# Holding back a group's gate products in two RWKV layers of a four-layer sequence model

## The chip, the cores and the metric

The program runs on one core of a Trainium2 chip. Its time is the device time of one execution in microseconds (us); where several runs are given, their median stands for them. The profile is of one execution of its own. The engines are called PE (TensorE, matrix products), DVE (VectorE), ACT (ScalarE), POOL (GpSimd) and SP (SyncE, which here only issues DMAs). Each works through its own queue in order.

## The reference

A batch of 16 sequences of 100 rows with 512 channels goes through four layers: a cross-attention (layer 0), an RWKV block (1), a transformer block with cross-attention and a feed-forward part (2), and a second RWKV block (3). All is float32. The change lies in the RWKV block, cut here to what matters:

```
xa = ln(x, ln1); sx = previous row - xa
xxx = tanh((xa + sx * maa_x) @ maa_w1).reshape(b, l, 5, 32) @ maa_w2     # five mixes
xk, xw, xv, xr, xg = xa + sx * (maa_stack + xxx)
w = exp(-exp(time_decay + tanh(xw @ td_w1) @ td_w2))
r, k, v = xr @ Wr.T, xk @ Wk.T, xv @ Wv.T
g = silu(xg @ Wg.T)                                # the gate
a = k[:, None] * v[None, :]                        # step by step along the rows
out = r @ (u * a + s);  s = a + w[:, None] * s
x1 = x + (groupnorm(out) * gn_w + gn_b) * g @ Wo.T
xc = ln(x1, ln2); sx2 = previous row - xc          # channel mixing
rr = sigmoid((xc + sx2 * ffn_maa_r) @ Wfr.T)
kk = square(relu((xc + sx2 * ffn_maa_k) @ Wfk.T))
return x1 + rr * (kk @ Wfv.T)
```

The gate `g` is needed only at the end of the time mixing, where it multiplies the normalised output ahead of `Wo`.

## The kernel before

The function `rwkv` writes one RWKV layer. The 16 sequences form four groups (0 to 3) of four, so a tile has 128 channels by 400 columns (four sequences of 100 steps), and there are four chunks of channels in a group. The recurrence is a scan along the 100 steps on DVE. It is cut into 128 units, 32 for each group and 8 for each chunk. The loop over `u` at the end of `rwkv` goes from -42 past 128, and each pass (called a slot here) writes the fixed work of one unit:

- `spread(u + 1)`: two pairs of products with `sel` on PE that lay out `v` in PSUM (`vb`), and a small copy from `s0r` on ACT. There are two `vb` tiles, so a spread waits for the scan two units before its own.
- `product(u)`: `vb` times `kr` on DVE.
- whatever an earlier slot has deferred (`slots.begin`), mostly readers of PSUM banks.
- `scan(u)`: two scans on DVE, and `a` times `rr` on POOL.
- in every other slot `gather`: eight products with `gat` into `acc`, and at a chunk's end its norm, spread over later slots.

Into these slots the rest is filled from a list, `pieces`. A piece has a cost in us, the first slot in which it may come, and a function that writes it. The list is gone through in order: `following(u)` gives the first piece whose slot has come, or the second half of a product chain that has begun. Each slot has a budget, `due` (2.37 in units 0 to 28, 2.75 up to unit 95, 3.5 then, 3.9 after the last unit, less a bit for the slot's fixed work), and pieces are written until it is used up. This fixes the order on PE, DVE, ACT and POOL, which keep the order in which instructions are written. The order of SP's DMAs is left to a scheduler.

`projections(g, base)` lists the pieces of a group's mixing, for group 1 at slot -10 and then every 32 slots: statistics (`stats`) on DVE, `root` on POOL, `normed` (the tiles `xn`) on ACT, `turned` (PE transposes, then `ext`, `sx`, `sm` and `xm` by ACT and POOL), `inner` (products with `maa_w1`, tanh into `z` and `tz`), `mixed` (products with `maa_w2`, read by DVE as `tm` and by POOL as `xj`), and the chains of four products with `Wk`, `Wv`, `Wr` and, last, with `Wg`. These last are the gates, `gate(co)` for four blocks of channels: tanh on ACT (`th`), then a product on DVE (`g`), then a store to DRAM (`dg`). `k`, `v`, `r` and the decay `w` are stored to DRAM too, and are loaded again by SP in `enter` and `repeat` in the layout of the scan (`kr`, `wr`, `rr`). `gates(C)` loads a chunk's gate (`gc`) once its scans are over. `through(("in", g))` in `enter` writes all of a group's pieces up to `r` that are still left.

`output` lists the `Wo` products of a group once its scans are over. `channel_stream` lists the channel mixing of groups 0 to 2 at slot 86, and of group 3 after the last unit.

Three PSUM banks serve all pieces in turn. When a bank's turn comes while its deferred reader is not written yet, the reader is written first.

The functions that the diff touches, and what calls them:

Of the kernel before, what the change touches and what calls it, by code (L numbers as in the profile page):

```python
# [16 lines left out]
NC = E // 128  # L17
# [18 lines left out]
def xattn_sequence(ctx: ExitStack, tc: tile.TileContext, d: dict, out: bass.AP):  # L36
# [599 lines left out]
    def rwkv(n, ws, next_weights, last):  # L636
# [6 lines left out]
        with ExitStack() as es:  # L643
# [88 lines left out]
            pieces = []  # L732

            begun = []
            added = {g: [] for g in range(NG)}
            cm = {}
            nws = {}

            def following(u):
                return next(  # L740
                    (p for p in pieces if (p[2] is begun[0] if begun else p[1] <= u)), None
                )

            def piece(us, fn, slot=-1000, tag=None):
                pieces.append((us, slot, fn, tag))

            def take(p):
                pieces.remove(p)
                p[2]()
                return p[0]  # L750
# [28 lines left out]
            def chain(us, slot, tag, before, ps, lhs, rhs, read):  # L779

                bank = []

                def half(i):
                    if i == 0:
                        for fn in before:
                            fn()
                        bank.append(slots.bank())
                        begun.append(second)
                    else:
                        begun.clear()  # L790
                    for c in (2 * i, 2 * i + 1):
                        mm(out=ps(bank[0]), lhsT=lhs(c), rhs=rhs(c), start=(c == 0), stop=(c == NC - 1))
                    if i:
                        read(bank[0])

                second = lambda: half(1)
                piece(us / 2, lambda: half(0), slot, tag)
                piece(us / 2, second, slot, tag)
# [54 lines left out]
            def projections(g, base):  # L853
# [6 lines left out]
                def store(t, c, tile):  # L860
                    nc.scalar.dma_start(out=to[t][c].rearrange("r p t -> (r p) t"), in_=tile)
# [48 lines left out]
                def inner(lo, hi):  # L910
                    p0, z = (0, "z0") if lo == 0 else (64, "tz")
                    rs = slice(p0, p0 + hi - lo)
                    chain(
                        2.7, late, None, soon, lambda ps: ps[rs, :T], lambda c: w1[:, c, lo:hi],
                        lambda c: st["xm"][:, c, :],
                        lambda ps: scalar.activation(st[z][rs, :], ps[rs, :T], AF.Tanh),
                    )
# [24 lines left out]
                def linear(f, w, co, read, tag):  # L942

                    before = mixes[f] if f >= 0 else soon
                    x = lambda c: xj[f][:, c, :] if f >= 0 else st["xm"][:, c, :]
                    chain(2.7, late, tag, before, lambda ps: ps[:, :T],
                          lambda c: w[:, c, co * 128 : (co + 1) * 128], x, read)

                def plain(f, w, t, co):
                    def read(ps):  # L950
                        out = stage(f"{t}_{nm}_{co}")
                        scalar.copy(out[:, :T], ps[:, :T])
                        store(t, co, out[:, :T])

                    linear(f, ws[w], co, read, ("in", g))
# [24 lines left out]
                def gate(co):  # L980
                    def read(ps):
                        th = two.tile([128, T], F32, tag="tm", bufs=4, name=f"th_{nm}_{co}")
                        scalar.activation(th, ps[:, :T], AF.Tanh, scale=0.5)

                        def product():
                            g2 = stage(f"g2_{nm}_{co}")[:, :T]
                            vector.scalar_tensor_tensor(g2, th, 1.0, ps[:, :T], ALU.add, ALU.mult)
                            store("g", co, g2)

                        slots.read_later(ps, product)  # L990

                    linear(4, ws["Wg"], co, read, None)
# [7 lines left out]
                    piece(0.45, lambda c=c: turned(c), base + 1)  # L1000
                late = base + 2
                mix = lambda fs, c: piece(0.75, lambda: mixed(fs, c), late)
                inner(0, 128)
                mix((0, 1), 0)
                mix((0, 1), 1)
                inner(128, 160)
                mix((0, 1), 2)
                mix((0, 1), 3)
                for c in range(NC):
                    plain(0, "Wk", "k", c)  # L1010
                    mix((2, 3), c)
# [7 lines left out]
                    plain(*((2, "Wv", "v", c + 2) if c < 2 else (3, "Wr", "r", c - 2)))  # L1019
                plain(3, "Wr", "r", 2)  # L1020
                plain(3, "Wr", "r", 3)
                for co in range(NC):
                    gate(co)

            def channels(g, slot):

# [83 lines left out]
                        i, slot, None, [], lambda c: st["kk"][:, c, :], lambda c: cm["Wfv"][:, c, :], read  # L1110
                    )

                def written(fn):
                    rest, pieces[:] = pieces[:], []
                    fn()
                    got, pieces[:] = pieces[:], rest
                    return got

                some = lambda fn, n: written(lambda: [piece(0.01, lambda i=i: fn(i), slot) for i in range(n)])
                root, normed = ln_apply(st, [xb[g * G + i] for i in range(G)], xn, nm)  # L1120
                return {
# [9 lines left out]
            def channel_stream(groups, slot):  # L1131

                got = []
                parts = [channels(g, slot) for g in groups]
                for k in ("stats", "normed", "turned"):
                    got += parts[0][k]
                for p, q in zip(parts, parts[1:] + [{"stats": [], "normed": [], "turned": []}]):
                    got += p["first"] + q["stats"] + p["second"] + q["normed"]
                    got += p["third"] + q["turned"] + p["fourth"]
                return got  # L1140
# [152 lines left out]
            UNITS = 32 * NG  # L1293
            u, due = -42, 0.0
            while u < UNITS + 6 or pieces or slots.due:
                slots.now = u
                g = (u + 10) // 32
                if u % 32 == 22 and g + 1 < NG:
                    projections(g + 1, u + 7)
                elif u % 32 == 22 and g + 1 == NG:  # L1300
                    pieces.extend(channel_stream(range(NG - 1), u + 7))
                elif u % 32 == 0 and u > 0:
                    if u == UNITS:

                        kept = max(len(pieces) - 4, 0)
                        for i in range(kept, len(pieces)):
                            pieces[i] = (pieces[i][0], u + 8, *pieces[i][2:])
                        own = channel_stream([NG - 1], u + 8)
                        pieces[kept:kept] = own[: G + 1]
                        pieces.extend(own[G + 1 :])  # L1310
                    output(g - 1, u + 7)
                if u == UNITS - 32 - 3:
                    cm.update(load(n, "Wfk", "Wfr", "Wfv"))
                if u >= UNITS and not nws and not any(p[3] == ("wo", NG - 1) for p in pieces):
                    nws.update(next_weights())
                unit = 0 <= u < UNITS
                if 0 <= u + 1 < UNITS:
                    spread(u + 1)
                if unit:
                    product(u)  # L1320
                slots.begin()
                if unit:
                    scan(u)
                C, at = u // 8 + 1, u % 8
                if 0 <= C < NC * NG:
                    if at == 4:
                        enter(C)
                    elif at == 6:
                        repeat(C, 1)
                        bonus(C, 0)  # L1330
                    elif at == 7:
                        bonus(C, 1)
                C = u // 8
                if 0 <= C < NC * NG and at == 2:
                    bonus(C, 2)
                if 0 < C <= NC * NG and at == 4:
                    gates(C - 1)
                if u % 2 and 0 <= (u - 3) // 2 < UNITS // 2:
                    gather((u - 3) // 2)

                due = min(due, 0.0) + (2.37 if 0 <= u < 29 else 2.75 if u < UNITS - 32 else 3.5 if u < UNITS else 3.9)
                due -= 0.45 * (u % 2) + 0.7 * (at in (2, 7)) if unit else 0.0
                for p in [p for p in pieces if p[0] == 0 and p[1] <= u]:
                    take(p)
                while due > 0:
                    p = following(u)
                    if p is None:
                        break
                    due -= take(p)
                u += 1  # L1350
# [359 lines left out]
    def load(layer, *names):  # L1710
        return {k: load_w(d[f"L{layer}_{k}"], f"l{layer}_{k}") for k in names}
# [75 lines left out]
```

## Time and profile before

| | us |
|---|---|
| median of three runs | 3452.1 (3450.18 to 3452.9) |
| profiled execution | 3447.39 |
| its span, first to last instruction | 3445.6 |
| PE busy in the span | 3121.5 |
| DVE busy | 1753.5 |
| POOL busy | 1373.2 |
| ACT busy | 977.3 |
| first scan of layer 1, last scan of layer 1 | 857.4, 1472.8 (its start) |
| first scan of layer 3, last scan of layer 3 | 2745.1, 3356.8 (its start) |

The mean granted clock of PE over the span is 0.942 of full speed.

How to read the lines that follow. A line of the timeline has the start in us from the span's beginning, the length, the engine, the source line, the operation, the tiles written and read, the shape and how many instructions were merged. In square brackets stands how long the engine was idle ahead of it, and what released it. Nearly all lines say L77 or L82, which are helpers that record every operation, so a group is told by its tiles. A product in float32 is recorded as two instructions. A line of a table of windows has the window, its length, then busy time and count of PE, PE's weight loads, DVE, ACT and POOL, then the granted clock, the share of DMA time and GB/s. A busy PE is not PE at its peak: with a halved clock or a late operand the recorded lengths grow.

### The profile page before, as it was taken

What the parts mean: (1) busy time and instruction counts of PE and PEld (TensorE: products, weight loads), DVE (VectorE), ACT (ScalarE), POOL (GpSimd) and SP (SyncE); (2) the same over time, 40 slices, a digit from 0 to 9 for tenths busy, and PEclk for the clock granted to TensorE, in tenths of its full rate; (3) what the DMA queues carried; (4) which work ended last, traced back from release to release, by engine and by line L of the source; (5) the groups of instructions that cost most, each with busy time, mean ns of one, the idle gap of its engine ahead of it and who ended that gap; (6) DMA issues with size and microseconds to landing.
All of it is one profiled execution on the core that took longest, in us unless ns stands there. A gap on an engine that the chain in (4) does not pass through costs nothing. (4 is left out here: it accounts for less than half of the span.)

```text
span 3445.6 us, 47937 instructions
## 1 busy us (share of the span) xinstructions
PE 3121.5 (91%) x18371; PEld 1422.0 (41%) x18371; DVE 1753.5 (51%) x3570; ACT 977.3 (28%) x1715; POOL 1373.2 (40%) x1036
## 2 busy tenths in 40 slices
PE   6989898868999989988999999879998899998997
PEld 3434443334333333334455555445553433333333
DVE  4777777732877766523333333320001287766661
ACT  1333233222233333321323222211111233423332
POOL 0444444443775765521212111220002377676551
PEclk8999999979999989999999999989998999998998
DMA  5010100013335353222000000010011343535321
GB/s 173 22 31 22 31 22 34 1 32 115 113 108 150 109 173 108 77 72 64 28 19 20 19 20 31 26 64 10 10 58 34 111 129 102 150 116 174 91 70 50
DMA packets 171374, 240.18 MB, mean 70 GB/s; under 512 B 27678, under 2 KB 139358, under 8 KB 171146
## 3 DMA queue, kind: packets, MB, share of 16 engines
q1 hardware_dynamic: 148106, 204.35, 19.9%
q10 hardware_dynamic: 23040, 32.78, 2.7%
q8 instruction: 144, 2.36, 0.3%
q14 instruction: 84, 0.69, 0.1%
HBM read 174.25 MB, written 36.04 MB: 61 GB/s over the span
## 5 line engine op out<-in xcount | busy, mean ns | idle before, releaser
L77 POOL TENSOR_TENSOR a<-a,rr 128x800 f32<-128x800 f32 x256 | 480.9, 1880 | 331.0 <-DVE a L77 212.0
L77 DVE TENSOR_TENSOR_SCAN a<-wr,vb 128x400 f32<-128x400 f32 x512 | 475.9, 971 | 20.7 <-PE acc L82 9.1
L77 DVE TENSOR_TENSOR vb<-vb,kr 128x792 f32<-128x792 f32 x256 | 250.1, 977 | 184.7 <-ACT vb L77 184.5
L77 DVE CUSTOM_DVE_ANT_0 junk<-l_sc,mask 100x361 f32<-100x361 f32 x512 | 272.9, 533 | 87.1 <-PE l_sc L82 70.5
L82 PE MATMUL vb<-vc,sel 32*128 32x396 f32 x1024 | 252.7, 565 | 3.3 <-DVE a L77 3.3
L77 DVE TENSOR_TENSOR pt<-l_sc,maskT 121x400 f32<-121x400 f32 x384 | 193.4, 566 | 89.6 <-PE l_sc L82 88.8
L77 ACT ACTIVATE pt<-pt 121x1600 f32<-121x1600 f32 x96 | 147.6, 1538 | 282.4 <-DVE pt L77 280.8
L1490 DVE CUSTOM_DVE_ANT_0 junk<-l2a_sc,mask 100x361 f32<-100x361 f32 x256 | 136.9, 535 | 173.0 <-PE l2a_sc L82 155.8
L1526 POOL TENSOR_TENSOR pa<-pt,pt 121x1600 f32<-121x1600 f32 x16 | 57.1, 3569 | 362.3 <-ACT pt L1521 362.3
L77 POOL TENSOR_TENSOR xj<-tm,ext 128x400 f32<-128x400 f32 x160 | 150.6, 961 | 110.9 <-DVE tm L77 110.1
L77 DVE SCALAR_TENSOR_TENSOR tm<-mm,vec,sx 128x400 f32<-128x400 f32 x160 | 95.7, 628 | 185.5 <-PE mm L82 149.4
L82 PE MATMUL k<-ct,l_k_w 128*128 128x361 f32 x512 | 173.3, 482 | 14.4 <-DMA ct<-in_ctxT 14.4
L1707 DVE TENSOR_TENSOR x<-pb,x 100x512 f32<-100x512 f32 x16 | 12.2, 760 | 335.4 <-DMA pb<-po 330.3
L77 POOL TENSOR_TENSOR pa<-pt,pt 121x1600 f32<-121x1600 f32 x32 | 114.7, 3583 | 165.0 <-ACT pt L77 165.0
L63 PE MATMUL h<-yTb,l_fc 128*128 128x400 f32 x512 | 174.5, 503 | 6.3 <-ACT yTb L229 6.3
L82 PE MATMUL v<-l_v_w,ct 128*121 128x512 f32 x384 | 175.5, 601 | 0.0
L63 PE MATMUL p<-l_proj,h 128*128 128x512 f32 x384 | 165.5, 592 | 0.0
L77 ACT COPY vb<-s0r 128x8 f32<-128x8 f32 x256 | 42.9, 168 | 407.8 <-PE vb L82 320.4
L82 PE MATMUL l_sc<-kz,qz 32*100 32x361 f32 x1024 | 116.7, 526 | 42.9 <-DVE pt L77 22.0
L82 PEld LDWEIGHTS vb<-vc,sel 32*128 32x128 f32 x1024 | 81.9, 191 | 154.0 <-issue 113.5
L63 PEld LDWEIGHTS h<-yTb,l_fc 128*128 128x128 f32 x512 | 97.7, 192 | 81.1 <-ACT yTb L229 8.3
L77 POOL TENSOR_TENSOR pa<-pa,pt 119x1600 f32<-119x1600 f32 x32 | 114.4, 3576 | 41.1 <-ACT pt L77 40.9
(258 smaller groups left out, 5174.2 us busy)
## 6 DMA issues: line engine op xcount, KB each, us to landing
kr<-dk SPq DMA_DIRECT2D x256, 100.0 KB
wr<-dw SPq DMA_DIRECT2D x256, 100.0 KB
rr<-dr SPq DMA_DIRECT2D x256, 100.0 KB
ct<-in_ctxT SPq DMA_DIRECT2D x32, 722.0 KB
dk<-k ACTq DMA_DIRECT2D x32, 200.0 KB
kc<-dk SPq DMA_DIRECT2D x32, 200.0 KB
dw<-wd ACTq DMA_DIRECT2D x32, 200.0 KB
dv<-v ACTq DMA_DIRECT2D x32, 200.0 KB
```

The source lines that it names most:

```text
L63: nc.tensor.matmul(out=ps, lhsT=lhs(c), rhs=rhs(c), start=(c == 0), stop=(c == n - 1))
L77: return lambda *args, **kw: tc.keep_in_program_order(op(*args, **kw))
L82: pin(nc.tensor.matmul(**kw))
L1490: nc.vector.tensor_tensor_reduce(out=junk, in0=ss[r][:L, :S2], in1=t["mask"], scale=-1.0, scalar=FLT_MAX, op0=ALU.add, op1=ALU.min, accum_ ...
L1526: nc.gpsimd.tensor_tensor(t["pa"], t["pt"][0], pt, ALU.add)
L1707: nc.vector.tensor_tensor(x, pb[:, i, :], x, ALU.add)
```

## The change

The four gate products of a group are no longer listed at the end of its own mixing. `projections` writes them into a list apart, `held`. The next call of `projections` puts them into its own pieces, one ahead of each of the first four parts: the first `inner`, two mixes, the second `inner`, two mixes. Their first slot is one before the new group's `base`, except for the first two that group 1 takes over, which may come at once. For the last group, `channel_stream` puts them behind its first `turned` pieces. Two budgets change. The helper `written` moves outward so that both callers reach it; it does what it did.

```diff
+            held = []
...
+            def written(fn):
+                rest, pieces[:] = pieces[:], []
+                fn()
+                got, pieces[:] = pieces[:], rest
+                return got
...
-                inner(0, 128)
-                mix((0, 1), 0)
-                mix((0, 1), 1)
-                inner(128, 160)
-                mix((0, 1), 2)
-                mix((0, 1), 3)
+                parts = [
+                    lambda: inner(0, 128), lambda: [mix((0, 1), c) for c in range(2)],
+                    lambda: inner(128, 160), lambda: [mix((0, 1), c) for c in range(2, 4)],
+                ]
+                for i, part in enumerate(parts):
+                    slot = base - 1 if g > 1 or i > 1 else -1000
+                    pieces.extend((p[0], slot, *p[2:]) for p in held[2 * i : 2 * i + 2])
+                    part()
...
-                for co in range(NC):
-                    gate(co)
+                held[:] = written(lambda: [gate(co) for co in range(NC)])
...
                 for k in ("stats", "normed", "turned"):
                     got += parts[0][k]
+                got += [(p[0], slot - 1, *p[2:]) for p in held]
+                held.clear()
...
-                due = min(due, 0.0) + (2.37 if 0 <= u < 29 else 2.75 if u < UNITS - 32 else 3.5 if u < UNITS else 3.9)
+                due = min(due, 0.0) + (2.22 if 0 <= u < 29 else 2.8 if u < UNITS - 32 else 3.5 if u < UNITS else 3.9)
```

In the built program, the order of the gate products around the slots in question is as follows. PE ahead of unit 0 keeps its order.

| slots | gate products before | after |
|---|---|---|
| 24 to 29 | all four of group 1 | the first two (28, 29) |
| 30, 31 | none | the third, half behind the transposes, half behind slot 31's gather |
| 35 | none | the fourth, between the second `inner` and the next mixes |
| 56 to 61 | all four of group 2 | the first two (60, 61) |
| 62, 63 and 66, 67 | none | the third; the fourth |
| 89 to 93 | all four of group 3 | the first two (92, 93) |
| 94, 95 and 96 | none | the third in halves behind the transposes and behind slot 95's gather; the fourth in 96 |

The pieces that follow come one to two slots later than before, and some of the channel mixing moves behind unit 125.

More of the change, by code (lines that the diff above doesn't have):

```diff
@@ L1111, in values @@
                     )
[L1113 to L1117, printed above, removed]
                 some = lambda fn, n: written(lambda: [piece(0.01, lambda i=i: fn(i), slot) for i in range(n)])
```

## Prediction

> **What bounds the kernel now.** I read the busy row and the clock row of the page, then a table of stages over the first RWKV layer, then the timeline at the places where that table loses time.
>
> ```profile
> PE 3121.5 (91%) x18371; PEld 1422.0 (41%) x18371; DVE 1753.5 (51%) x3570; ACT 977.3 (28%) x1715; POOL 1373.2 (40%) x1036
> ...
> PEclk8999999979999989999999999989998999998998
> ```
> ```profile
> 857.00:966.00 109.00, 104.87 (x427) 39.75 (x428) 91.91 (x115) 31.57 (x72) 78.52 (x63) 0.95 0.39 117
> 966.00:1005.00 39.00, 33.58 (x129) 13.25 (x128) 25.70 (x34) 14.41 (x30) 30.54 (x27) 0.86 0.33 95
> 1005.00:1111.00 106.00, 105.63 (x433) 40.84 (x432) 79.95 (x101) 32.54 (x70) 65.35 (x51) 0.97 0.46 136
> ...
> 1262.00:1305.00 43.00, 32.14 (x98) 13.05 (x96) 21.40 (x30) 17.84 (x34) 27.99 (x27) 0.72 0.60 194
> ```
>
> The first number after the window is its length, the next TensorE's busy time, and the share below 1 is the granted clock. In 1005 to 1111 TensorE is busy 105.63 of 106: it is the bound. In 966 to 1005 (group 1's mixing to group 2's) and 1262 to 1305 (the last group to the channel mixing) it is not: 5.4 and 10.9 us idle, at a clock of 0.86 and 0.72. The timeline of the first place:
>
> ```profile
> 970.92 0.93 PE L82 MATMUL vb<-vc,sel 32*128 32x396 f32 x4
> 971.79 0.88 PE L82 MATMUL acc<-a,gat 128*32 128x400 f32 x8
> 972.60 1.61 PE L82 MATMUL mm<-xj,l_Wg 128*128 128x400 f32 x4
> 974.14 0.93 PE L82 MATMUL vb<-vc,sel 32*128 32x396 f32 x4
> ...
> 978.24 0.56 PE L85 MATMUL mm<-ident,xn_a 100*128 100x100 f32 x4 [1.04 <-ACT ext L77]
> 981.42 1.70 PE L82 MATMUL mm<-rk,ones 128*128 128x400 f32 x2 [1.75 <-POOL rk L77]
> 985.85 5.21 PE L82 MATMUL mm<-xm,maa_w 128*128 128x400 f32 x8 [1.23 <-POOL xm L77]
> ```
> ```profile
> 982.00:986.00 4.00, 2.77 (x11) 0.36 (x9) 2.02 (x4) 2.51 (x4) 4.00 (x6) 0.50 0.87 267
> 986.00:990.00 4.00, 4.00 (x6) 1.98 (x7) 0.52 (x1) 0.00 (x0) 4.00 (x4) 0.50 0.69 164
> ```
>
> Starts give prices: a spread 0.87, a gather 0.81, half a product chain 1.54 (a whole one 2.88 by other rows). Transposes, shift, mix and the `maa_w` product follow each other through ACT, POOL and PE, and PE waits at each step.
>
> **The change, part by part.** No matrix product, vector operation or byte of DMA is added. I write slot u for unit u's pass of the loop. The built order shows what moves:
>
> (a) Ahead of unit 0, PE's order is the same. On VectorE the four statistics of group 1 stood behind all four gate products; now the last two stand behind `g` 1, and `th` 3 on ScalarE stands behind the four `xn`.
>
> ```profile
> 835.06 0.69 DVE L77 BATCH_NORM_STATS2 st_a<-x 100x6 f32<-100x512 f32 x1
> 838.44 0.23 POOL L77 TENSOR_SCALAR ve_a<-mv_a 100x4 f32<-100x4 f32 x1 [21.72 <-DVE mv_a L77]
> 840.44 2.93 ACT L77 ACTIVATE xn_a<-x,shift_a,rstd_a 100x512 f32<-100x512 f32 x4 [5.90 <-POOL shift_a L77]
> 841.31 0.43 PE L85 MATMUL mm<-ident,xn_a 100*128 100x100 f32 x1 [7.37 <-ACT xn_a L77]
> 843.28 0.61 ACT L77 ACTIVATE kc<-kc,vec 128x400 f32<-128x400 f32 x1
> ```
> `g` 1 ends at 829.8; two statistics at 0.86 end at 831.5; root and shift take 2.0 (838.44 to 840.44); `xn` runs 833.5 to 836.4 beside the last gate chains. Then `th` 3 (0.5), `g` 3 (0.57), its store's issue (0.33) are ahead of `kc`, which starts at 837.9 instead of 843.28: everything behind it, `ext` to unit 0, comes 5.4 earlier. Unit 0's loads don't hold it: the DMA share is 0.19 in 838 to 842 and 0.08 from 840. Two layers: 10.8.
>
> (b) At units 30 and 62. Before, from the spread at 970.92 to the end of the first half `Wk` product at 1006.3 are 35.4 us, for PE work of 6 spreads (5.2), 3 gathers (2.4), a half gate (1.5), 16 transposes (1.6), the `ones` product (0.9), `maa_w` (4.3), 8 mixes (3.5), the centring (0.8), half a `Wk` (1.5): 21.7, so 13.7 lost. The same stretch at the other three places (unit 62, and both in layer 3) loses 10.7 to 13.0; mean 12.6. After, three gates more stand in the stretch, and the preceding slots are as much emptier. I walk it from 970.92 with the same durations: gate 1 whole until 975.5; spread 976.4; the third transpose waits for gate 1's bank (`th` 976.4, `g` 977.0), the fourth for `ext` (978.4), end 978.8 as before. Half of gate 2 fills until 980.3, the spread until 981.2; `ones` waits 0.7 for `rk`, gather and gate 2's other half end at 985.1, a spread at 986.0. `xm` on POOL comes at 986.3 to 989.0, so `maa_w` ends at 989.7. Mixes, `maa_w`'s rest, centring, spread, `mean`, gather: 999.8; gate 3 until 1002.7; spread, four mixes (waiting for `tm` behind scan 36) and half a `Wk`: 1009.0. That is 38.1 for 31.6 of work (two spreads, a gather, `mean`, two and a half gates more): 6.5 lost. Gain 6.1 a place, but some 4.4 at unit 30: in group 0 VectorE is busy 92 of 109 us (first row of the stages) and PE not quite the bound, so of the 6.7 us of gates taken out of it I let 5 come back. Two layers: 21.0.
>
> (c) At unit 94.
> ```profile
> 1274.74 0.43 PE L85 MATMUL mm<-ident,xn_1b 100*128 100x100 f32 x1 [4.50 <-ACT xn_1b L77]
> ...
> 1289.89 3.54 PE L82 MATMUL mm<-xk_1b,l_Wfk 128*128 128x400 f32 x4 [4.57 <-POOL xk_1b L77]
> ```
> Four half gates (5.8) move behind the transposes, into the second wait. But the statistics come one unit later (behind `g`, a product and scan 94: 3.5 more), so the first wait grows from 4.5 to 8. The walk, from slot 93's spread: spread, gather and half a gate to 3.2, spread 4.1; scan 94 ends at 6.4, the statistics 9.8, root (on POOL behind `a` 94 and `rk`) 11.6, `xn` from 12.4, transposes 15.2; half a gate, spread, `ones`, gather, half a gate 20.8; spread and gate 3 to 24.6. POOL's eight mixes of 0.93 run from 19.2 to 26.7, so the first half of `Wfk` doesn't wait (26.1); spread 27.0, gather behind `a` 95 at 29.4, half a `Wfk` 30.9. Before, slot 97's spread begins at 37.6 (1304.53) with four half chains (5.5) more, but without that spread and gather (1.7): equal work is at 34.7 against 37.6. With 5.4 less ahead of it, 8.3. Two layers: 16.6.
>
> (d) The budgets (2.22 for 2.37 in units 0 to 28, 2.8 for 2.75) split chains otherwise; half a chain alone costs 0.2 more than in a whole. Summed by these prices, units and tail together hold 528 us of PE work by either order; some 6.8 us move behind unit 125. There one half product fills the wait of 4.2 for POOL's last `gc`: 1.5, two layers 3.
>
> (e) Queues. SP's order changes: `gc` loads move ahead of `kr` loads, as late as a gate's store. `Wr`'s last store comes 3 units later (unit 59 and 91); its row must land before unit 64 and 96, over 20 us later, against a store and 13 issues of 0.4: nothing. From group 1 on `gc` waits for buffers that `Wo` frees, as now.
>
> Sum: 51.4 at full clock. The clock's price: the rows of 982 to 990 show 0.50 though no PE wait there reaches 2 us. The Trainium skill, TensorE: Matmul & The Clock Gate, Part 1, puts the half rate behind an idle window of some 3.4 us. By that rule nothing in (b) drops after the change, and only (a) and (c) would pay. The row decides: the clock dropped in a stretch that was thinly filled (7.1 busy of 9), and the walk still has 2.4 us of waits between transposes. From 980 to 991 the granted clock is 0.53: 10.3 us at half rate, at most 5.1 of work lost, and each of the six places has such a row. I charge it whole at (c), with its wait of 8, and one in two at (b): 2 x 5.1 + 4 x 2.6 = 20.6. Gain 30.8.
>
> The profiled run took 3447.4 (span 3445.6, the rest outside it); the sums are made on it, and taken from the median of 3452.1, which is 4.7 longer with the same work: **3421.3**.
>
> **Rivals.** *Full clock*: no dip at these places, 3452.1 - 51.4 = 3400.7. For it: the gates are steady work; against: (a) keeps thin stretches. *Only the start gains*: the stalls return elsewhere since the mixing begins later by a unit, 3452.1 - 10.8 = 3441; for it, (c)'s longer first wait. *No effect*: 3452; against, PE's 7.37 is no other engine's limit. *Slower*: a held gate's `g` stands before a scan in VectorE's queue, and its `th` now behind four `sm` (gate 2) or two table loads (gate 3) on ScalarE. Behind the scan wait POOL's `a`, and the second next spread with all of PE. In the walk scan 32 frees that spread 0.8 before PE asks. Twelve such waits; beyond the 0.8 each us is on the path, so 2.6 more eat the 30.8, and at 3.6 more it is 3464.5. Such waits show 2.1 now (57.1 over 27), which leaves it the smaller case.
>
> **How the numbers follow.** 0.2% (6.9 us) is what a measurement here can tell from no change. Likeliest, with its dips up or down: 0.58, own range 3408 to 3438. Full clock 0.07, only the start 0.09 (of it some within 0.2%), no effect 0.08, slower 0.18. So faster 0.72, same 0.10, slower 0.18; the range 3400 to 3459 leaves out the far end of slower and little below.
>
> **What would show it.** (a) the first scan 5 us earlier; (b) the waits for `rk` and `xm` mostly gone, and a higher clock; (c) the wait for `xn_1b` longer, that for `xk_1b` under 1. It is wrong if `g` waits over 100 us in total, or if the clock in 966 to 1005's counterpart stays under 0.86.

## The result and the profile after

| | before | changed |
|---|---|---|
| median, us | 3452.4 | 3444.5 |
| ratio (95% interval) | | 0.9975 (0.9964 to 0.9986) |
| profiled execution, us | 3447.39 | 3446.68 |
| its span, us | 3445.6 | 3444.8 |
| PE busy in the span, us | 3121.5 | 3117.8 |

Both medians are of 20 executions. The change is real but small: 8.6 us of 3452 (4.8 to 12.4), where 30.8 were forecast. Executions of one kernel spread by some 10 us either way; the two profiled executions happen to lie 0.7 apart. So sizes below come from the ratios, as (1 - ratio) x 3452, and the traces tell the place.

The page of the changed kernel, busy row and clock row:

```profile
PE 3117.8 (91%) x18371; PEld 1421.2 (41%) x18371; DVE 1754.7 (51%) x3570; ACT 977.3 (28%) x1715; POOL 1373.0 (40%) x1036
...
PEclk8999999979999899899999999989998899999999
```

Its stages of layer 1 (columns as in the table of windows before):

```profile
851.00:965.00 114.00, 109.25 (x466) 42.25 (x466) 101.42 (x126) 40.21 (x87) 87.23 (x68) 1.00 0.39 119
965.00:1005.00 40.00, 37.56 (x140) 13.41 (x140) 27.05 (x36) 12.14 (x25) 32.56 (x30) 0.91 0.30 89
1005.00:1111.00 106.00, 97.92 (x412) 37.09 (x410) 77.07 (x97) 31.32 (x67) 62.19 (x49) 0.97 0.46 138
...
1160.00:1262.00 102.00, 93.67 (x386) 35.94 (x385) 71.28 (x85) 28.34 (x62) 59.11 (x45) 0.95 0.47 139
1262.00:1305.00 43.00, 33.74 (x128) 15.10 (x127) 24.56 (x35) 17.94 (x36) 28.57 (x27) 0.84 0.52 167
```

and of the kernel before the one stage that was not shown:

```profile
1160.00:1262.00 102.00, 102.00 (x423) 39.71 (x424) 75.08 (x90) 29.96 (x67) 63.16 (x48) 0.98 0.50 148
```

The two places that the prediction looked at are better: in the mixing's stretch PE is busy 37.56 of 40 at a clock of 0.91 (before 33.58 of 39 at 0.86), in the channel mixing's at 0.84 instead of 0.72. The two stretches behind the mixings, where PE was the bound, no longer are: 97.92 of 106 and 93.67 of 102, against 105.63 and 102.00. In these, 16 us of PE's time went missing in one layer, against 0.4 before. The starts of scans say it in time:

| start of unit's scan, us | before | changed | lead |
|---|---|---|---|
| layer 1, unit 0 | 857.4 | 851.4 | 6.0 |
| unit 28 | 968.3 | 952.2 | 16.1 |
| unit 36 | 1009.5 | 989.8 | 19.7 |
| unit 62 | 1125.4 | 1114.8 | 10.6 |
| unit 76 | 1193.7 | 1192.3 | 1.4 |
| unit 94 | 1273.1 | 1271.9 | 1.2 |
| unit 127 | 1472.8 | 1463.2 | 9.5 |
| layer 3, unit 0 | 2745.1 | 2737.0 | 8.1 |
| unit 36 | 2898.2 | 2879.5 | 18.7 |
| unit 94 | 3160.4 | 3159.4 | 1.0 |
| unit 127 | 3356.8 | 3351.6 | 5.2 |

The lead at unit 36 is there in both layers, and it is larger than what the prediction's steps (a) and (b) ask for by then (5.4 and 4.4; in layer 3, 3.7 of it stood before the layer began). It is nearly gone at unit 76. (Of unit 28's lead a part is only work put off by the smaller budget: in experiment 2, which has the budgets alone, a lead of 7.0 over the first scan at unit 30 has shrunk to 0.2 at unit 36.)

PE at the first mixing transition of the changed kernel, the counterpart of the timeline shown before:

```profile
961.11 1.25 PE L85 MATMUL mm<-ident,xn_a 100*128 100x100 f32 x12
963.12 0.56 PE L85 MATMUL mm<-ident,xn_a 100*128 100x100 f32 x4 [0.76 <-ACT ext L77]
963.70 1.61 PE L82 MATMUL mm<-xj,l_Wg 128*128 128x400 f32 x4
...
966.30 0.94 PE L82 MATMUL mm<-rk,ones 128*128 128x400 f32 x2
...
970.74 3.70 PE L82 MATMUL mm<-xm,maa_w 128*128 128x400 f32 x8 [0.29 <-POOL xm L77]
```

The waits of 1.75 for `rk` and 1.23 for `xm` are 0 and 0.29, and `maa_w`'s eight products take 3.70 instead of 5.21, at full clock. At the channel transition:

```profile
1279.87 0.43 PE L85 MATMUL mm<-ident,xn_1b 100*128 100x100 f32 x1 [8.19 <-ACT xn_1b L77]
...
1295.02 1.58 PE L82 MATMUL mm<-xk_1b,l_Wfk 128*128 128x400 f32 x4
```

the first wait is 8.19 (forecast: 8) and the second none (forecast: under 1). So the waits at these places are as the walks had them. What took the gain back are waits that the kernel before doesn't have. The first, at unit 46, seen on PE, POOL and SP:

```profile
1046.78 1.70 PE L82 MATMUL mm<-rk,ones 128*128 128x400 f32 x2 [5.78 <-POOL rk L77]
```
```profile
1041.04 1.03 POOL L77 TENSOR_TENSOR gc<-gc,og 128x400 f32<-128x400 f32 x1 [3.92 <-PE vb L82]
...
1045.68 1.04 POOL L77 TENSOR_TENSOR rk<-rc,kc 128x400 f32<-128x400 f32 x1
```
```profile
1028.96 4.21 SPq L837 DMA_DIRECT2D x<-ox  x6
...
1037.25 0.37 SPq L1275 DMA_DIRECT2D gc<-dg  x1
```

The gate's load `gc` stands behind six stores of `Wo`'s rows and eight loads on SP and is issued at 1037.25. POOL waits for it until 1041.04 (the profile puts the wait down to `vb`, whose products end at the same moment; experiment 7 issues the gates' loads by ACT and the wait is gone; it moves a row load too, but that one is not late here), and two mixes, an `a` and `rk` queue behind it, so PE's `ones` product waits 5.78. The second, at unit 76, on PE, DVE and SP:

```profile
1187.49 0.84 PE L82 MATMUL mm<-z,maa_w2a 32*128 32x400 f32 x4
1192.46 4.39 PE L82 MATMUL mm<-xj,l_Wk 128*128 128x400 f32 x8 [4.14 <-DVE ox L77]
```
```profile
1192.12 0.29 DVE L77 TENSOR_TENSOR ox<-mm,ox 128x128 f32<-128x128 f32 x1 [5.36 <-DMA ox<-x]
```
```profile
1184.13 1.65 SPq L837 DMA_DIRECT2D x<-ox  x2
...
1188.33 2.47 SPq L832 DMA_DIRECT2D ox<-x  x4
```

DVE adds `Wo`'s fourth row tile to the rows `ox`. These rows are loaded just ahead of use, DVE stands idle for 5.36 with a scan next in its queue, and a bank stays taken, so PE waits too. In SP's built order that load was far ahead in the kernel before (group 0's is row 72 of the queue and group 1's row 73); the change left the one in place and moved the other to row 202:

```
72   DMACopy ox_0_3<-x  32x128 x4      before and changed
73   DMACopy ox_1_3<-x  32x128 x4      before
202  DMACopy ox_1_3<-x  32x128 x4      changed
```

The traces have it so. SP's first row loads of layer 1, before and then changed:

```profile
743.27 5.00 SPq L823 DMA_DIRECT2D ox<-x  x8
```
```profile
743.53 2.47 SPq L832 DMA_DIRECT2D ox<-x  x4
```

What makes the load late is a store. It reads rows 68 to 99 of the group's last sequence, and `Wo`'s third row tile is stored into rows 0 to 83 of the same tile. Where the load is written ahead of that store, it depends on no result of the layer, and the scheduler puts it at the layer's head. Where it is written behind the store, SP has to wait for the store first; in the built program of the changed kernel such a wait stands just ahead of row 202. The lines show the round trip: the third tile's rows are stored at 1184.13, the load follows at 1188.33, and DVE adds at 1192.12. The kernel before writes load and use of groups 0 and 1 in one slot (44 and 76), and yet ahead of the store. In the changed kernel the four tiles of group 1 begin in slots 71, 72, 74 and 75 instead of 72, 73, 75 and 76, and the third is stored before the fourth begins.

The totals of DVE's waits, before and then changed:

```profile
DVE ox L77 <- DMA ox<-x: 10.6, 2, 5.3
```
```profile
DVE ox L77 <- DMA ox<-x: 20.4, 4, 5.4
```

The line has the idle time, how often, and the longest. Two waits (group 2's rows at unit 108, one in each layer) are in both kernels; the other two are new. That is as many as there are loads written behind such a store: over both layers two in the kernel before and in experiment 5, four in the changed kernel and in experiments 7 and 11, six in experiments 1, 6 and 8, and none in those that write the load earlier (9, 10, 13 to 16). (Experiment 2 has four, and waits for three.)

### The profile page after: what moved, and what is told of

The parts are those of the page before. It is cut to its first block, busy times and chain, and to the rows that moved or that the text cites. A ratio compares the mean times of both kernels' runs of the same rounds, so it can differ in the third digit from the quotient of the medians.

```text
span 3444.8 us, 47891 instructions
## 1 busy us (share of the span) xinstructions
PE 3117.8 (91%) x18371; PEld 1421.2 (41%) x18371; DVE 1754.7 (51%) x3570; ACT 977.3 (28%) x1715; POOL 1373.0 (40%) x1036
## 5 line engine op out<-in xcount | busy, mean ns | idle before, releaser
L82 PE MATMUL k<-ct,l_k_w 128*128 128x361 f32 x512 | 172.5, 480 | 13.5 <-DMA ct<-in_ctxT 13.5
```

The lines of the kernel that those rows point to most:

```text
L82: pin(nc.tensor.matmul(**kw))
```

## The experiments

Gains are given against the kernel before, as (1 - ratio) x 3452, with the interval of the ratio. "Old budgets" are 2.37 and 2.75, "new" ones 2.22 and 2.8.

**1. All gates held, old budgets.**

```diff
-  (2.22 if 0 <= u < 29 else 2.8 if ...
+  (2.37 if 0 <= u < 29 else 2.75 if ...
```

> The gates are held as in the changed kernel, but the budgets stay at 2.37 and 2.75. Theory A, waits of the new order (a held gate pushes every later piece of its group back, and the Wo rows, the chunk loads and the last mixes then meet SP's and POOL's queues badly): the lead of 20 us at unit 36 of layer 1 is there and is lost again by unit 76 and unit 125 as in the changed kernel, 3438 to 3452. Theory B, the budgets (2.22 puts off pieces of group 0, 2.8 draws the later ones forward, and that makes the waits): the lead is kept, 3420 to 3432.

Measured 3457.0, ratio 1.0018 (1.0008 to 1.0028): 6 slower than before, and outside both expectations. The new budgets are not what makes the waits; under the old ones the held gates fare worse. DVE waits for `ox` in every group but the last (41.3 in total, six times, up to 7.8), and at unit 95 PE waits 7.4 for `rk`, which stands behind eight mixes on POOL.

**2. The budgets alone**, in the kernel before (2.22 and 2.8, gates not held).

> The kernel before with the budgets 2.22 and 2.8 alone, gates not held. Theory A: about as before, 3445 to 3460. Theory B: the waits seen in the changed kernel (the ones product for rk at unit 47 near 6 us, the POOL mixes at unit 125) come without the held gates, and it is 12 to 22 slower, 3464 to 3474.

Measured 3502.3, 1.0150 (1.0134 to 1.0167): 52 slower, far outside both expectations. The budgets are a gain only together with the held gates; the prediction had them at 3 us of gain. Where the 52 go was not found: of the waits in its trace, PE's for `xm` stand at 25.9 (12.0 before) and those behind `ox` at 13.6 (none before), and both layers lose.

**3. Only group 0's gates held**, old budgets.

```diff
-  held[:] = written(lambda: [gate(co) for co in range(NC)])
+  if g == 0:
+      held[:] = written(lambda: [gate(co) for co in range(NC)])
+  else:
+      for co in range(NC):
+          gate(co)
```

> Only the gates of group 0 are held, and written into group 1's mixing; the gates of groups 1 to 3 stay behind their own group's chains; old budgets. Prediction's step (a): the first scan of each layer 5 to 8 us earlier and unit 7 to 9's half clock gone, 3441 if it stays. Theory A: the lead at unit 28 of 12 to 16 us is there, and what is left at the end is less than 6 a layer. Rival, the start is paid back before unit 30: as before, 3452.

Measured 3429.7, 0.9942 (0.9920 to 0.9964): 20.0 faster, more than the 3441 expected. Step (a) had 10.8 for both layers. Its profiled execution lies 17 above its median, so no size is read from that. A second part of the gain was looked for in the half clock behind the start. The kernel before runs at a clock of 0.57 in 884 to 896 (units 7 to 9), the changed one at full clock in the same units:

```profile
884.00:896.00 12.00, 12.00 (x34) 4.56 (x38) 6.82 (x9) 0.68 (x3) 7.34 (x5) 0.57 0.44 129
```
```profile
878.00:890.00 12.00, 12.00 (x59) 4.53 (x59) 10.65 (x14) 2.39 (x7) 9.93 (x8) 1.00 0.58 176
```

But the changed kernel has other budgets there. Experiment 5, with the start and the budgets of this one, has the half clock nearly whole, and its lead over the first scan does not grow in units 0 to 36 of that layer:

```profile
882.00:894.00 12.00, 12.00 (x37) 4.36 (x36) 6.64 (x10) 0.83 (x3) 6.80 (x5) 0.58 0.47 126
```

In this experiment's own trace it lasts 3.4 us instead of 10.2 and the lead grows by 3.3. So the half clock does not go with the held gates every time, and what makes 20.0 of 10.8 is open.

**4. Only group 3's gates held**, old budgets (the condition is `g == NG - 1`).

> Only the gates of group 3 are held, and written behind the transposes of the channel mixing; groups 0 to 2 as before; old budgets. Prediction's step (c): 8.3 at full clock less 5.1 for the clock at each of two places, so 3446, with the wait for xn_1b near 8 and that for xk_1b under 1. Theory A: the gain at unit 96 is there and the last mixes at unit 125 take it back: 3450 to 3458. A rival, the clock: no gain at unit 96 either, since the wait of 8 costs as much in half clock as the fill brings.

Measured 3434.2, 0.9955 (0.9941 to 0.9970): 15.5 faster, near step (c)'s 16.6 at full clock and not its 6.4 with the clock's charge. Both waits were as forecast.

**5. Groups 0 and 3 held, 1 and 2 not**, old budgets.

> The gates of group 0 and of group 3 are held, those of groups 1 and 2 are not; old budgets. If the two gains measured apart add up: 22.6 + 18.1 less than before, 3412. If each was partly one run's luck with the clock, or if both save the same idle time: 3425 to 3432. In either case the changed kernel would be slower than this by what it pays for groups 1 and 2.

Measured 3416.6, 0.9901 (0.9884 to 0.9918): 34.2 faster, nearly the sum of the two (35.5), and 26 better than the whole change.

**6. Only groups 1 and 2 held**, old budgets: step (b) by itself.

> Only the gates of groups 1 and 2 are held, so only the mixing at units 30 and 62 changes; old budgets. Prediction's step (b): 21.0 less 10.4 for the clock, 3442. Theory A': the transition gains at units 30 to 36 as predicted, but the order behind it makes the row load of the Wo rows (ox) stand behind the chunk loads on SP, with some 7.6 of DVE idle at units 44 and 76 in each layer (30 together, less the gain of 21): about 3460. By difference (all held with old budgets +4.7, start -22.6, channels -18.1): +45, 3497.

Measured 3461.1, 1.0023 (1.0011 to 1.0035): 7.9 slower, as theory A' had it (its place and its size; the cause is the store described above, not a place behind the chunk loads). The place is the one of theory A', on DVE

```profile
1048.67 0.29 DVE L77 TENSOR_TENSOR ox<-mm,ox 128x128 f32<-128x128 f32 x1 [7.64 <-DMA ox<-x]
```

and on PE, 7.74 behind it:

```profile
1040.34 0.94 PE L82 MATMUL mm<-z,maa_w2a 32*128 32x400 f32 x4
1049.02 5.33 PE L82 MATMUL mm<-xj,l_Wk 128*128 128x400 f32 x8 [7.74 <-DVE ox L77]
```

The eight `Wk` products behind it take 5.33 instead of 2.95, at a granted clock of 0.55 (1049 to 1054.4): such a wait is paid again in the clock. The difference by subtraction (45 slower) was wrong: experiment 1 loses 34 more than its parts added up (20.0 + 15.5 - 7.9, against -6.2), of which the wait of 7.4 at unit 95 is the largest part seen; in 4 and 6 no wait for `rk` is over 1.9. The rest of the 34 was not traced.

**7. The changed kernel with two loads by ACT.** The fourth row tile's load and the gates' load are issued by ACT and not by SP.

```diff
-  nc.sync.dma_start(out=chunks[C]["g"], ...)
+  nc.scalar.dma_start(out=chunks[C]["g"], ...)
-  x[i] = rows_in(f"ox_{n}_{g}", g, i)                       # issued by SP
+  x[i] = rows_in(f"ox_{n}_{g}", g, i, nc.scalar if i == 3 else nc.sync)
```

> The changed kernel with two loads issued by ACT and not by SP: the fourth row tile of each group's Wo rows (ox) and the gates (gc). Theory A' (SP's queue makes the late waits): DVE's wait for ox at unit 75 (5.4) and POOL's for gc at unit 46 (3.9, and 5.8 of PE behind it) go, some 10 to 12 a layer: 3421 to 3426. Rival, PE would only wait elsewhere, since the mixes on POOL behind it are as late: 3438 to 3446.

Measured 3432.5, 0.9941 (0.9922 to 0.9961): 20.4 faster than before, 11.7 better than the change. Half of the expectation, between its two ranges: POOL's order is the same instruction for instruction, `gc` no longer waits in it,

```profile
1040.81 1.88 POOL L77 TENSOR_TENSOR a<-a,rr 128x800 f32<-128x800 f32 x1
1042.64 1.04 POOL L77 TENSOR_TENSOR gc<-gc,og 128x400 f32<-128x400 f32 x1
```

and PE's wait for `rk` behind it is 2.08 instead of 5.78. But DVE still waits for `ox` (21.3 in total, 5.5 the longest). By ACT the row load is issued no earlier: the store that it waits for is the same.

**8. Experiment 1 with the same two loads by ACT.**

> All gates held with the old budgets, and the same two loads by ACT. Theory A': DVE's waits of 7.6 for ox at units 44 and 76 go, 30 over two layers: 3427. Rival, the loss lies in the clock or in the fill of the units: 3450 to 3460.

Measured 3458.0, 1.0018 (1.0007 to 1.0029): nothing gained. ACT's queue shows why:

```profile
1035.69 2.06 ACTq L1275 DMA_DIRECT2D gc<-dg  x4
1040.16 2.51 ACTq L832 DMA_DIRECT2D ox<-x  x4
```

`bring` writes the load when its product chain begins. At slot 44 (and 76) `gates` forces all that is left of `Wo`, and by then the third tile's store is written. So the load waits for the store on ACT's queue as it did on SP's. That load and use are written in one slot is not what holds it: they are in the kernel before, too.

**9. Experiment 7, and the fourth row tile's load written one chain earlier.**

```diff
-  before + [lambda i=i: bring(i)],
+  before + [lambda j=j: bring(j) for j in ((0,), (1,), (2, 3), ())[i]],
```

> The changed kernel with both loads of the run before by ACT, and the fourth row tile's load (ox) issued with the third's, one product chain earlier. Theory: what is left of DVE's wait for ox at unit 76 (5.5, and 4.9 of PE) goes, 5 in each layer with what it does to the clock: 3432.5 less 8 to 12, 3421 to 3425. Rival, the wait is only handed on: 3430 to 3435.

Measured 3416.5, 0.9902 (0.9885 to 0.9919): 33.8 faster than before, 25 better than the change and 5 under what was expected. Written with the third tile's load, the fourth's stands ahead of the store, and goes to the layer's head. At unit 76 DVE and PE go on without a wait:

```profile
1183.78 0.84 PE L82 MATMUL mm<-z,maa_w2a 32*128 32x400 f32 x4
1184.55 2.95 PE L82 MATMUL mm<-xj,l_Wk 128*128 128x400 f32 x8
```

and the stretches behind the mixings are PE's again:

```profile
1001.00:1103.00 102.00, 97.62 (x414) 37.20 (x412) 77.12 (x96) 31.61 (x68) 64.57 (x52) 0.98 0.50 145
...
1150.00:1249.00 99.00, 96.16 (x409) 37.07 (x410) 72.67 (x87) 29.60 (x65) 62.55 (x48) 0.97 0.54 158
```

**10. Experiment 1 with the row load written earlier, by SP** (the edit of 9 alone).

> All gates held, old budgets, and only the fourth row tile's load issued one chain earlier, by SP. At slots 44 and 76 the gates' loads force what is left of the Wo products into one slot, so that load and use stood 7 to 8 apart in time with DVE waiting. Theory: four waits of 7 go, 3457 less 25 to 30, 3427 to 3432, with the stall of 13 at unit 95 left. Rival, SP's queue holds the earlier load as long: 3450 to 3457.

Measured 3428.5, 0.9938 (0.9921 to 0.9955): 21.4 faster than before, 27.6 better than experiment 1, as the theory had it. This is the load moved alone, on its own queue. "One chain earlier" in the text is far earlier in time: the loads of groups 0 to 2 are issued together at the layer's head,

```profile
745.64 8.07 SPq L832 DMA_DIRECT2D ox<-x  x12
```

Unit 95's stall stayed.

**11. Groups 0 and 3 held, with the new budgets.**

> Gates of groups 0 and 3 held, those of 1 and 2 not, with the changed kernel's budgets. The step from here to the changed kernel is what holding the middle gates does under its own budgets. If the budgets alone hurt here as they do without any held gate (50 slower): near 3465, and holding the middle gates gains 20. If they are neutral, as predicted: 3417, and holding the middle gates costs 28.

Measured 3466.0, 1.0048 (1.0029 to 1.0066): 16.6 slower. Under the changed kernel's own budgets, holding the middle gates as well gains 25 (from here to the change), as the first expectation had it; under the old ones the same step, from experiment 5 to 1, costs 40 (and 8 from the kernel before, experiment 6). DVE waits for `ox` here too (23.5, four times).

**12. Experiment 5 with PE's wait filled.** Eight products whose result is not used, ahead of the channel mixing's first transposes.

```diff
   ps = slots.bank()
+  for i in range(8 if c == 0 and g == 0 else 0):
+      mm(out=ps[:, :T], lhsT=ws["Wo"][:, 0, :128], rhs=ws["Wo"][:, 1, :T], start=True, stop=True)
```

> Gates of groups 0 and 3 held, old budgets, and eight products whose result is not used (5.8 us of PE) written ahead of the channel mixing's first transposes, into PE's wait of 8.2 for xn_1b at unit 94; added work, same output. The clock's charge (the wait of 8 brings half clock afterwards, 5.1 lost): the dip behind it goes and it is 4 to 10 faster than without, 3407 to 3413. Rival, the dip doesn't come from this wait or isn't on the path: 3415 to 3419.

Measured 3418.2, 0.9910 (0.9889 to 0.9930): as without the fill, as the rival had it. The wait was cut from 8.19 to 2.63:

```profile
1258.79 5.64 PE L82 MATMUL mm<-l_Wo 128*128 128x400 f32 x16
1267.06 0.30 PE L85 MATMUL mm<-ident,xn_1b 100*128 100x100 f32 x1 [2.63 <-ACT xn_1b L77]
```

but the clock fell all the same, for 7 us (0.52 in 1268 to 1275) where experiment 5 has at least 9 (0.50 in 1268 to 1277):

```profile
1268.00:1275.00 7.00, 6.40 (x23) 3.96 (x22) 0.00 (x0) 3.81 (x6) 3.29 (x4) 0.52 0.49 131
```
```profile
1268.00:1277.00 9.00, 3.85 (x17) 3.11 (x18) 4.05 (x7) 5.02 (x8) 4.35 (x9) 0.50 1.03 310
```

From scan 93 to scan 101 it takes 47.0 and 48.0 (the two layers) against 46.0 and 46.0 in experiment 5. So a shorter dip gained nothing here, with the fill's own 5.6 us added. The time of these two runs alone would leave room for a gain of a few us; the stretch itself leaves none. A dip that was removed altogether was not to be had by this fill.

**13. The kernel before with both loads moved** (edits of 7 and 9).

> The kernel before, gates not held, old budgets, with both loads moved as in the ninth run (by ACT, the fourth row tile's one chain earlier). Its DVE shows no wait for ox inside the scans and POOL none for gc, so if these two waits are what the change brought with it, this is as before, 3446 to 3454. Rival, the moved loads are a gain of their own that has nothing to do with the change: 3420 to 3432.

Measured 3441.4, 0.9975 (0.9962 to 0.9988): 8.6 faster, between the two. The kernel before had a late row load of its own, the two waits of 5.3 at unit 108, and these go. But its ACT now waits 19.1 ahead of `tz` for the gates' loads in its own queue, which experiment 9 does not. So of the 25 that the loads bring to the changed kernel, 9 are the kernel's own and 16 the change's only by subtraction; the row load moved by itself was not tried in the kernel before, and may be worth more than 9 there.

**14. Only groups 1 and 2 held, row load written earlier**, by SP.

> Only the gates of groups 1 and 2 held (sixth run, 8.6 slower than before), old budgets, and the fourth row tile's load issued one chain earlier, by SP. This is the prediction's step (b) without the late load: by the walk 21.0 at full clock, 10.4 with the clock's charge, so 3431 to 3442. Rival, the middle transitions gain nothing: 3450 or more.

Measured 3432.5, 0.9936 (0.9919 to 0.9952): 22.1 faster than before, in the expected range, and 30 better than experiment 6. The add that waited 7.64 there has no wait:

```profile
1042.60 0.27 DVE L77 TENSOR_TENSOR ox<-mm,ox 128x128 f32<-128x128 f32 x1
```

Less the 9 or so of experiment 13 for the kernel's own late load, step (b) comes to some 13.5, or to less if that load is worth more.

**15. Groups 0 and 3 held, both loads moved.**

> Gates of groups 0 and 3 held, old budgets, both loads moved as in the ninth run. The order in the middle is that of the kernel before and shows no late load there, so 3414 to 3418, as without. Rival, loads by ACT free SP's queue for the chunk loads: 3405 to 3411.

Measured 3426.5, 0.9923 (0.9907 to 0.9940), outside both expectations, and 8 slower than experiment 5 as far as the overlapping intervals tell. Its ACT waits 19.1 in total ahead of `tz`, put down to the gates' loads in its own queue, as in experiment 13; experiments 9 and 16 have no such wait ahead of `tz`. Whether this is the cause was not tried.

**16. All gates held, old budgets, both loads moved.**

> All gates held, old budgets, both loads moved. Against the tenth run (3428.5, the row load alone moved) this has the gates' loads by ACT; POOL waited 6.4 over four gc loads there: 3420 to 3428. What is left against the ninth run (3416.5) is the stall of 13 at unit 95 under the old budgets. Rival: ACT holds its own work behind a load's wait, 3428 to 3440.

Measured 3414.4, 0.9888 (0.9869 to 0.9908): 38.7 faster than before and 6 under what was expected, the best of all though not told apart from 5 and 9. What is left in it is unit 95:

```profile
1280.27 1.70 PE L82 MATMUL mm<-rk,ones 128*128 128x400 f32 x2 [7.40 <-POOL rk L77]
```

## Why the prediction was right and wrong

**Faster, yes; by a quarter of the forecast.** 8.6 instead of 30.8, inside the range, outside the likeliest case's own.

**The step that failed is (e)**, "Queues", which ended in "nothing". It followed the moved gates' stores and loads, and compared `gc` with `kr`, but not with the stores of `Wo`'s rows, and it left out `Wo`'s own row loads, which the moved pieces reorder. Both became late: `gc` behind six stores (POOL 3.9, PE 5.8), and the fourth row tile's load behind the third tile's store (DVE 5.4, PE 4.1 at unit 76 under the new budgets; 7.6 at units 44 and 76 under the old). Measured: 25 (experiment 9 against the change), of which some 16 are the change's own, by subtraction. Without these the change would stand near 3452 - 8.6 - 16 = 3427 by this estimate, inside the likeliest range of 3408 to 3438.

**(d) failed with it.** It summed PE's work, found it equal by either order, and put the budgets at 3. Alone they cost 52, with held gates they gain 15 (experiment 1 to the change). What a sum of work does not hold is the order of stores and loads, which a budget changes too: group 0's row load comes behind its store in experiment 2, and in experiment 1 but not in the change. That is a part of it; the rest stays open.

**(a) was right in place, and too small.** The first scan is 6.0 earlier in layer 1 and 8.1 in layer 3 (4.4 of it won in layer 3 itself, which already begins 3.7 earlier); over both layers it is worth 20.0 (12.4 to 27.6), or 18.6 by experiments 4 and 5. From the first `Wk` product to the first scan, the traces with group 0's gates held take 75.8 to 78.6 us and the others 81.8 to 83.0, so the walk's 5.4 is confirmed; what the rest of the 20.0 is stays open (experiment 3).

**(b) was right in its walk and wrong in the end.** At the place shown `rk` and `xm` come nearly without wait and the clock is up. By itself it is 7.9 slower; with the row load moved it is 22.1 faster, so the loss is (e)'s. Net of the kernel's own late load some 13.5 are left, between the 10.4 with and the 21.0 without the clock's charge.

**(c) was right**, waits of 8.19 and none. It is worth 15.5, or 14.2 by experiments 3 and 5. The charge for the clock, 5.1 a place, was too large here: the 6.4 that it left lies outside experiment 4's 10.4 to 20.4. Experiment 12 shortens the dip and gains nothing.

**The sum.** Each part alone, (b) net of late loads, gives 20.0 + 15.5 + 13.5 = 49, close to the 51.4 at full clock, but by luck: (a) is twice its size and (b) a third under. The charge of 20.6 for the clock is refuted at (c) and not tested at (b). And the parts don't add up: all together with the loads moved are worth 33.8 (9) or 38.7 (16), of which 8.6 or more are the kernel's own loads. What takes the difference is seen at unit 95 in 16 and was not settled for 9. So it is luck, too, that experiment 9 comes so near the forecast 30.8.

**The rivals.** *Only the start gains*, "the stalls return elsewhere since the mixing begins later by a unit", gave 3441 and came nearest: stalls do return. But they are others than the one it named, the start alone is worth 20.0 and not 10.8, and the channel transition gains as well, so its number is luck. *Slower*, a `g` in front of a scan: the waits for `g` grew from 57.1 to 74.9 in total, under the bound of 100; it is not where the time went. *Full clock* fell, *no effect* too.

## What to carry to other kernels

When pieces of an order written by hand are moved, follow those that shift with them, not only those that are moved. Ask of each load whether it still stands ahead of the stores into the tile that it reads: behind one of them it waits for a round trip through memory, and no other queue helps. Write such a load by a piece of its own, ahead of the store, and compare the place of every load in the DMA queue's built order, not only of those that the diff names. A gain at the place that one looked at, and a lead in the scans that shrinks later, are told apart only by a table of leads along the whole run.

## What was not expected of the hardware

- The clock fell in experiment 12 with no wait over 2.63 in front of it. The Trainium skill, TensorE: Matmul & The Clock Gate, Part 1, puts half rate behind an idle window of some 3.4 us. The trace agrees with the length: from the end of the fill at 1264.4 to the fall at 1267.9 are 3.5 us. PE was busy for 0.5 of these, all of it transposes. The kernel before's fall at 980.2 (in the prediction's rows) says more: in the 3.4 us ahead of it PE was busy for 1.9, 0.9 of them a spread's products (978.74 to 979.67), and the clock fell. So the window need not be idle throughout; how busy it may be is not settled here.
- Executions of one kernel differ with the clock that they are granted, with nothing changed: those of the changed kernel at a mean clock of 0.949 to 0.951 took 3431 to 3438, those at 0.944 took 3446 to 3449. Which of the two brings the other is not shown. The spread is wider than most of the effects that were looked for here.
- A row load moved from SP to ACT is no gain by itself (experiment 8, 1.0018 as without): what counted was whether it was written ahead of the store that it must otherwise wait for (experiment 10, 27.6 us).
